# One VectorE transpose of the second input row moved behind the first LayerNorm's statistics, in a two-layer graph kernel on one core

## The chip, the cores and the metric

The kernel runs on one NeuronCore of a Trainium2 chip. A core has five engines that run side by side, each working through its own list of instructions in order: TensorE (matrix products, in the profile PE, its weight loads PEld), VectorE (DVE), ScalarE (ACT), GpSimd (POOL) and SyncE (SP), which here issues the DMA transfers.[...] The metric is the device time of one execution in microseconds (us); all times below are in us unless ns is written.

## What is computed

There are 128 graphs of 128 nodes with 512 features each (`x`), and an adjacency matrix of 128 x 128 for each (`adj`). Two layers follow each other, each with a residual and a LayerNorm without gain:

```python
# layer 0: graph attention, 8 heads of 64 units
feats  = einsum('bnf,hfu->bhnu', X, W)
dense  = leaky_relu(e_self[..., :, None] + e_neigh[..., None, :], 0.2)
att    = softmax(dense + NEG_BIG * (1 - A))
out    = relu(einsum('bhij,bhju->bhiu', att, feats) + b)
x      = layernorm(x + out)
# layer 1: two hypergraph convolutions, Dn H Be H^T (x W^T), with a layer_norm between
h = relu(hypergraph_conv(x, adj, W1, b1))        # 512 -> 1024
h = layer_norm(h, gamma, beta)
y = hypergraph_conv(h, adj, W2, b2)              # 1024 -> 512
x = layernorm(x + (y + x))
```

"The first LayerNorm" below is the one at the end of layer 0.

## The kernel before

The kernel takes two graphs at a time, a pair, so there are 64 pairs (0 to 63); g = 0, 1 is the graph within the pair, called row 0 and row 1 below. The products of the large weight matrices are done in a form with seven half-size products instead of eight (`chain`, line 314; `rows_product`, line 469, whose matmuls stand at L476), and sums of blocks on the other engines.

The order of all instructions is written out by hand. Every step is a small function with a lag and a time; `at` (line 311) and `step` (line 304) collect them. For pair p the step gets the time (p + lag) * 38.6 plus its own, all steps of all pairs are sorted by this number (line 1169), and they are issued in this order. The numbers aren't measured times; they only fix the order on each engine. In the first pairs and the last two, tables (`first`, line 1106, and line 1151) replace some of them. With lags from 0 to 4, a period of the loop works on five pairs at a time: it loads and transposes pair m, makes the features of pair m-1, the attention and first LayerNorm of pair m-2, and so on. A period is named below by the pair whose `propagate` product (pz) begins it.

These are the steps around the change, in the order in which VectorE meets them late in a period:

- `load_blocks` (line 114, L121): SyncE loads the input rows of a pair in 32-row blocks into `xb` (one buffer).
- `x_transpose` (line 370, the instruction is L373): VectorE transposes `xb` into `xT`, one instruction of 128x512 for each row g. GpSimd's `x_sums` (L458, tile xS) and the feature products (pf) read it in the next period.
- `attend` (line 662, L665, tile pav): TensorE's attention products; its weights are eT, which `e_transpose` (L630) makes on VectorE from the loaded blocks eb.
- `attended` (L679, L680): VectorE divides by the softmax sums; `add_bias` (L689): GpSimd adds b0.
- `residual` (L696): VectorE's relu and addition of x; `moments` (L704, L705): statistics and mean and variance, per row.
- `rstds` (L710, L712): VectorE adds epsilon (vea), GpSimd raises to the power -0.5 (rsa), once for both rows.
- `first_shift` and `first_output` (L728, L730, L737): ScalarE applies the LayerNorm.
- `masked` (L579, GpSimd), `leaky` (L595, ScalarE), `largest` (L601, VectorE): the scores of the next pair, behind it.
- `y_sum` (L879 on VectorE, L877 on ScalarE): sums of layer 1's second product, of an earlier pair; one with pyY stands ahead of, one with pyW behind the moved transpose.
- `edges` (L409 to L416) and `r_evict` (L440): VectorE makes hT and the propagation matrix R.
- `propagate` (L760, pz): TensorE multiplies the normalized rows y by R; `z_evict` (L772): ScalarE copies pz to zT, row 0 and then row 1; `z_sums` (L783): GpSimd's four differences zS.
- `hidden` (L795, phX, phY, phW): TensorE's product with W1; its first one reads zT of row 0.
- `h_rstd` (L944 to L947, tile rsh, GpSimd) and `y_scale` (L951, VectorE): the inner layer norm's factor, behind zS on GpSimd.

The steps that the change reorders have these times: `x_transpose` of row 1 has lag 0 and 30.65, from pair 2 on; `residual` of row 1 has lag 2 and 30.7, and `rstds` lag 2 and 30.8. In the same period these belong to pairs m and m-2.

Of the kernel before, what the change touches and what calls it, by code (L numbers as in the profile page):

```python
# [20 lines left out]
def kernel(  # L21
# [289 lines left out]
    def at(lag, time, fn, *args, since=0, until=PAIRS):  # L311
        steps.append((lag, time, fn.__name__, range(since, until), fn, args))
# [63 lines left out]
        )  # L376

    at(0, 26.15, x_transpose, 0, since=2)
    at(0, 30.65, x_transpose, 1, since=2)

    def x_transpose_first(p, s):
        s["px"] = [bank(f"px_{p}_{g}") for g in range(2)]
# [100 lines left out]
    def feature(s, i, to, start):  # L483
# [4 lines left out]
          feature, FW, since=2)  # L488
# [724 lines left out]
```

## Time and profile before

| | |
|---|---|
| median of three runs | 2532.51 (2531.58 to 2532.85) |
| the profiled execution | 2532.93 |
| its span, first to last instruction | 2531.1 |
| granted TensorE clock, mean | 0.998 |
| VectorE, ScalarE, GpSimd busy | 80%, 61%, 71% |
| HBM traffic, mean over the span | 135 GB/s |
| idle of VectorE until xb has landed (L373) | 57.1 in 60 waits |
| idle of GpSimd until vea is there (L712, rsa) | 98.8 in 51 waits |
| idle of ScalarE until the mean is there (L728) | 64.8 in 62 waits |

Idle time of an engine that isn't the bottleneck costs nothing by itself. A period of the loop takes 38.7 from one pz to the next, so 64 pairs with the filling and emptying of the pipeline make up the span. What a change within a period is worth is therefore read from one period's timeline, and multiplied by the number of pairs.

### The profile page before, as it was taken

How to read it: one execution, taken by the hardware profiler on the slowest of the kernel's cores; microseconds unless marked ns; L12 is line 12 of the kernel's file. 1: busy time of each engine (PE TensorE's matmuls, PEld its weight loads, DVE VectorE, ACT ScalarE, POOL GpSimd, SP SyncE). 2: the span in 40 equal slices, each digit the busy share in tenths (PEclk: the TensorE clock that was granted, in tenths of full speed). 3: DMA queues.
4: the chain of work that ended last, by engine and by line, in shares of the span. 5: the costliest groups of instructions: out<-in, count | busy, mean ns of one | idle time of the engine just before them, and what ended most of it. 6: DMA issues, size and time to landing. Idle time of an engine off the chain costs nothing.

```text
span 2531.1 us, 48862 instructions
## 1 busy us (share of the span) xinstructions
PE 2500.8 (99%) x16225; PEld 2253.8 (89%) x16225; DVE 2014.2 (80%) x4580; ACT 1539.8 (61%) x4481; POOL 1794.0 (71%) x2060
## 2 busy tenths in 40 slices
PE   7999999999999999999999999999999999999998
PEld 5898999998999989989989999899899898988997
DVE  7878778778778788787787887887877877778765
ACT  4565665755756656657556566566575565665753
POOL 5767776776677677767776777777677767776774
PEclk9999999999999999999999999999999999999999
DMA  6444445445444444454454544444544444444431
GB/s 186 131 138 137 141 134 147 131 133 142 139 136 140 139 140 140 128 151 130 131 149 130 142 140 139 142 136 128 150 129 135 148 136 137 139 135 142 136 115 51
DMA packets 432747, 345.04 MB, mean 136 GB/s; under 512 B 153176, under 2 KB 382064, under 8 KB 432496
## 3 DMA queue, kind: packets, MB, share of 16 engines
q1 hardware_dynamic: 429024, 337.46, 45.3%
q10 hardware_dynamic: 3472, 4.47, 0.6%
q8 instruction: 129, 2.11, 0.3%
q14 instruction: 122, 1.00, 0.1%
HBM read 239.08 MB, written 102.73 MB: 135 GB/s over the span
## 4 chain that ended last, share of the span: by engine, by line
PE 92%; DVE 2%; DMA 2%; ACT 1%; issue 1%; SPq 1%; POOL 1%; DVEq 0%; POOLq 0%; ACTq 0%
PE phX L795 18%; PE pyX L476 16%; PE phW L795 9%; PE pfX L476 8%; PE pav L665 8%; PE pyW L476 8%; PE phY L795 4%; PE pq L961 4%; PE pz L760 4%; PE pfW L476 4%; PE pyY L476 4%; PE pfY L476 2%; PE pd L432 1%; PE pf L513 1%; DMA xb<-in_x_dram 1%
## 5 line engine op out<-in xcount | busy, mean ns | idle before, releaser
L332 ACT COPY py<-pyX 128x257 f32<-128x257 f32 x189 | 70.6, 374 | 539.4 <-PE pyX L476 523.4
L795 PEld LDWEIGHTS phX<-zS,w_sb 128*128 128x128 f32 x3072 | 363.1, 192 | 32.9 <-issue 31.5
L795 PE MATMUL phX<-zS,w_sb 128*128 128x128 f32 x3072 | 374.3, 275 | 2.3 <-POOL xS L458 1.3
L848 POOL TENSOR_TENSOR sq<-sq 128x512 f32<-128x512 f32 (+2 forms) x384 | 343.4, 894 | 20.3 <-ACT sq L836 0.2
L579 POOL TENSOR_TENSOR nb<-nb,neg 128x512 f32<-128x512 f32 x256 | 318.3, 1276 | 6.9 <-DMA nb<-rd 6.9
L609 ACT ACTIVATE nb<-nb,nm 128x128 f32<-128x128 f32 x1024 | 319.4, 391 | 4.6 <-DVE nm L601 0.4
L595 ACT ACTIVATE nb<-nb,ft 128x128 f32<-128x128 f32 x1020 | 317.3, 389 | 6.8 <-POOL nb L579 6.8
L601 DVE TENSOR_REDUCE nm<-nb 128x4 f32<-128x512 f32 x256 | 174.7, 683 | 174.5 <-ACT nb L595 105.8
L712 POOL TENSOR_TENSOR rso<-veo,mhalf 128x2 f32<-128x2 f32 x63 | 44.1, 700 | 371.2 <-DVE veo L710 371.2
L825 ACT ACTIVATE h<-h,vecs 128x128 f32<-128x128 f32 x768 | 245.0, 392 | 53.6 <-DVE h L810 53.6
L665 PEld LDWEIGHTS pav<-ft,eT 128*128 128x128 f32 x2048 | 243.8, 191 | 17.2 <-issue 12.2
L665 PE MATMUL pav<-ft,eT 128*128 128x65 f32 x2048 | 246.3, 273 | 0.0
L476 PE MATMUL pyX<-w_sb,hS 128*128 128x257 f32 x1008 | 242.5, 382 | 0.0
L476 PE MATMUL pyW<-w_sb,hS 128*128 128x256 f32 x1008 | 238.6, 378 | 1.4 <-DVE y L879 1.4
L476 PE MATMUL pyX<-w_sb,h 128*128 128x257 f32 x1008 | 239.4, 379 | 0.5 <-ACT py L332 0.5
L476 PEld LDWEIGHTS pyW<-w_sb,hS 128*128 128x128 f32 x1008 | 190.6, 189 | 29.1 <-issue 1.8
L689 POOL TENSOR_TENSOR y<-y,b_bc 128x512 f32<-128x512 f32 x128 | 162.6, 1271 | 68.2 <-DVE y L680 68.2
L476 PEld LDWEIGHTS pyX<-w_sb,h 128*128 128x128 f32 x1008 | 186.4, 190 | 25.5 <-ACT py L332 0.9
L476 PEld LDWEIGHTS pyX<-w_sb,hS 128*128 128x128 f32 x1008 | 186.1, 190 | 24.3
L373 DVE STREAM_TRANSPOSE xT<-xb 128x512 f32<-128x512 f32 x124 | 138.0, 1114 | 57.1 <-DMA xb<-in_x_dram 57.1
L951 DVE SCALAR_TENSOR_TENSOR y<-y,rsh,bw_bc 128x512 f32<-128x512 f32 x126 | 148.6, 1218 | 19.0 <-POOL rsh L947 18.5
L630 DVE STREAM_TRANSPOSE eT<-eb 128x512 f32<-128x512 f32 x252 | 162.2, 679 | 0.5 <-DMA eb<-ed 0.4
(174 smaller groups left out, 5726.8 us busy)
## 6 DMA issues: line engine op xcount, KB each, us to landing
nb<-rd SPq DMA_DIRECT2D x127, 512.0 KB
ed<-nb SPq DMA_DIRECT2D x126, 512.0 KB
eb<-ed SPq DMA_DIRECT2D x504, 128.0 KB
x<-in_x_dram SPq DMA_DIRECT2D x64, 512.0 KB
out_dram<-o SPq DMA_DIRECT2D x63, 512.0 KB
xb<-in_x_dram SPq DMA_DIRECT2D x248, 128.0 KB
a<-in_adj_dram SPq DMA_DIRECT2D x64, 128.0 KB
w<-in_adj_dram SPq DMA_DIRECT2D x128, 64.0 KB
```

The source lines that it names most:

```text
L476: nc.tensor.matmul(to[:, :n], lhs[:, k, :], rhs[:, k, :n], start=bool(start) and k == 0, stop=(k == nk - 1), skip_group_check=True,)
L579: nc.gpsimd.tensor_tensor(t, t, neg[:, :, None, :].to_broadcast([P, NB, HH, B]), op=ALU.add)
L595: nc.scalar.activation(t, t, AF.Prelu, bias=s["ft"][:, g, h, 0:1], alpha=SLOPE)
L601: nc.vector.tensor_reduce(s["nm"][:, g, hs], scores(p, s, g, hs).rearrange("p b h j -> p h b j"), AX.XY, ALU.max, negate=True,)
L609: nc.scalar.activation(t, t, AF.Exp, bias=s["nm"][:, g, h:h + 1])
L630: nc.vector.transpose(s["eT"][:, g, hs, :].rearrange("p h (b i) -> p h b i", b=NB), s["eb", g][:, :, hs, :].rearrange("p b h j -> p h b j"),)
L665: nc.tensor.matmul(t[:, h * (U + 1):(h + 1) * (U + 1)], s["eT"][:, g, q * HH + h, :], s["ft"][:, g, q * HH + h, 2:], start=True, stop=True,)
L689: nc.gpsimd.tensor_tensor(s["y"][:, g, :], s["y"][:, g, :], b0_bc, op=ALU.add)
L795: nc.tensor.matmul(to[:, m * N:(m + 1) * N], w[:, k, m * P:(m + 1) * P], rhs[:, k, :], start=bool(start) and m == 0 and k == 0, stop=(k == ...
L825: nc.scalar.activation(dst[:, k, :], src[:, k, :], AF.Relu, bias=b1_sb[:, c:c + 1])
L848: nc.gpsimd.tensor_tensor(t[:, :n, :], t[:, :n, :], t[:, n:2 * n, :], op=ALU.add)
L951: nc.vector.scalar_tensor_tensor(t, t, s["rs", "h"][:, g:g + 1], bw_bc.rearrange("p (j c) -> p j c", j=2), op0=ALU.mult, op1=ALU.add,)
```

## The change

One number: the time of `x_transpose` for row 1 goes from 30.65 to 30.85, which is behind `residual` of row 1 (30.7) and `rstds` (30.8) and ahead of everything that followed them.

```diff
     at(0, 26.15, x_transpose, 0, since=2)
-    at(0, 30.65, x_transpose, 1, since=2)
+    at(0, 30.85, x_transpose, 1, since=2)
```

On VectorE, the four instructions L696, L704, L705 and L710 of pair m-2 now stand ahead of the one L373 of pair m, where they stood behind it. This happens for the transposes of pairs 3 to 63, thus beside the LayerNorms of pairs 1 to 61; pair 2's transpose has its own time in the table `first`, which isn't changed, and pairs 62 and 63 have no transposes beside them. The lists of the other engines stay in the same order.

## The prediction

> **What bounds the kernel now.** I read the page first, then TensorE's list of waits, the timeline of all engines over one ordinary pair (pair 25 of 0 to 63), and last TensorE's timeline at the same two places of other pairs.
>
> ```profile
> PE 2500.8 (99%) x16225; PEld 2253.8 (89%) x16225; DVE 2014.2 (80%) x4580; ACT 1539.8 (61%) x4481; POOL 1794.0 (71%) x2060
> ```
> ```profile
> PE phX L795 <- ACT zT L772: 4.0, 6, 1.6
> ```
>
> TensorE is busy 99% of the span, and the waits put down to it come to some 25 us, nearly all at the two ends of the run. The only one that recurs is the first product of `hidden` (phX) waiting for ScalarE's eviction zT, six times. But a busy matmul record can contain a wait, because its end is modelled, so I go by starts. In this timeline of pair 25 the columns are start, length, engine, line, operation, names, sizes, count and, in brackets, the idle time before with its releaser:
>
> ```profile
> 1018.64 0.42 DVE L879 TENSOR_TENSOR y<-py,pyY 128x257 f32<-128x257 f32 x1
> ...
> 1018.98 1.10 DVE L373 STREAM_TRANSPOSE xT<-xb 128x512 f32<-128x512 f32 x1
> ...
> 1020.01 0.65 DVE L696 SCALAR_TENSOR_TENSOR y<-y,x 128x512 f32<-128x512 f32 x1
> ...
> 1021.64 0.17 DVE L710 TENSOR_SCALAR vea<-mva 128x2 f32<-128x2 f32 x1
> ...
> 1021.89 0.70 POOL L712 TENSOR_TENSOR rsa<-vea,mhalf 128x2 f32<-128x2 f32 x1 [1.92 <-DMA sd<-sr]
> 1022.11 0.42 DVE L879 TENSOR_TENSOR y<-py,pyW 128x256 f32<-128x256 f32 x1 [0.30 <-PE pyW L476]
> ...
> 1025.75 1.95 PE L760 MATMUL pz<-R,y 128*128 128x128 f32 x16
> ...
> 1027.01 1.31 ACT L772 COPY zT<-pz 128x512 f32<-128x512 f32 x2
> ...
> 1027.64 2.05 PE L795 MATMUL phX<-zT,w_sb 128*128 128x128 f32 x16
> ```
>
> The transpose sits ahead of the second residual, and the chain residual, statistics, vea, GpSimd's power, ScalarE's outputs and leaky activations runs without a break into the copy of pz. That copy starts at 1027.01 although the first half of pz (8 of 16 matmuls) is done near 1026.8. So the phX start, 1.89 after pz, is late: first wait, A. A product of this form takes 1.79 from start to start elsewhere in the timeline. The second wait, B, is at the first attention product (pav), which needs VectorE's transposes eT. VectorE, then TensorE:
>
> ```profile
> 1045.61 1.29 DVE L630 STREAM_TRANSPOSE eT<-eb 128x512 f32<-128x512 f32 x2
> ```
> ```profile
> 1046.45 1.97 PE L665 MATMUL pav<-ft,eT 128*128 128x65 f32 x16
> 1048.26 1.11 PE L476 MATMUL pfX<-w_sb,xT 128*128 128x264 f32 x4
> ```
>
> The first of the two eT ends near 1046.3, just before pav starts, and pav takes 1.81 to the next group; the later pav of a pair, whose eT lies ready, takes 1.73 (1013.11 to 1014.84). Now pair 26, then pair 10, where the block load xb landed late:
>
> ```profile
> 1064.47 1.95 PE L760 MATMUL pz<-R,y 128*128 128x128 f32 x16
> 1066.40 0.82 PE L795 MATMUL phX<-zT,w_sb 128*128 128x128 f32 x5
> ...
> 1085.18 1.95 PE L665 MATMUL pav<-ft,eT 128*128 128x65 f32 x16
> 1086.96 1.11 PE L476 MATMUL pfX<-w_sb,xT 128*128 128x264 f32 x4
> ```
> ```profile
> 432.43 1.11 DVE L373 STREAM_TRANSPOSE xT<-xb 128x512 f32<-128x512 f32 x1 [1.64 <-DMA xb<-in_x_dram]
> ...
> 444.20 1.95 PE L760 MATMUL pz<-R,y 128*128 128x128 f32 x16
> 446.64 0.60 PE L795 MATMUL phX<-zT,w_sb 128*128 128x128 f32 x3 [0.49 <-ACT zT L772]
> ...
> 465.42 1.90 PE L665 MATMUL pav<-ft,eT 128*128 128x65 f32 x16
> 467.15 1.11 PE L476 MATMUL pfX<-w_sb,xT 128*128 128x264 f32 x4
> ```
>
> Pair 26: A grows to 1.93, B shrinks to 1.78, and pz to the next pz is 38.70 against 38.72 in pair 25. Pair 10: A is 2.44, B falls to its floor of 1.73, and the period is 39.16 (next pz at 483.36). So what A gains or loses, B gives back until its wait is used up: in ordinary pairs the period is held by B. Its chain is: end of pz, ScalarE's second zT copy (waits for pz, not for statistics), four GpSimd zS differences, the power rsh, VectorE's y_scale at 1032.59, then VectorE almost without a gap to eT.
>
> **What the Trainium skill says.** "Perfetto Trace Analysis", Identifying the Most-Contended Engine: matmul busy share does not tell how close TensorE is to its limit, since its records are pipelined; the 99% above with two hidden waits in it agrees. "SBUF — State Buffer", Who interferes with whom: a VectorE instruction with two SBUF inputs and a GpSimd one that reads SBUF exclude each other, and the first to start holds the port to its end. The trace agrees: the residual of row 0, beside GpSimd's squares, takes 1.34 (at 1014.10), that of row 1 takes 0.65. Pair 62, which has no transposes behind it, has the changed order already, and shows both the price and the effect (GpSimd's m beside the residual, against 0.19 elsewhere; ScalarE's copy):
>
> ```profile
> 2452.47 0.57 POOL L939 TENSOR_TENSOR m<-y 128x1 f32<-128x1 f32 x1 [1.25 <-DVE y L879]
> ```
> ```profile
> 2460.15 0.58 ACT L772 COPY zT<-pz 128x512 f32<-128x512 f32 x1 [0.72 <-PE pz L760]
> ```
>
> There ScalarE waits 0.72 for pz, and phX follows pz by 1.79 (2459.06 to 2460.85): A's floor.
>
> **The change part by part.** No instruction is added or removed; on VectorE one transpose moves behind four instructions (residual, two of statistics, vea) in 61 of 64 pairs, 1 to 61. TensorE, ScalarE, GpSimd and SyncE keep their orders.
>
> 1. *Four instructions earlier.* The residual starts when the transpose did, 1.03 earlier (1020.01 − 1018.98). It needs GpSimd's bias addition, which ends at 1018.81, 0.17 before; so no new wait. GpSimd's two m and the mask (1019.15 to 1019.97) are held by the residual to about 1019.6, end near 1020.5, and are clear of the power, now due near 1020.86. Gain to the power: 1.03; bounds 0.35 (residual doubled to 1.34, as row 0's is) and 1.03.
> 2. *Ordinary pairs, 54.* Everything to the zT copy comes earlier, the copy then waits for pz, A falls from 1.89 to 1.79 as in pair 62, and the phX group behind it, whose first matmul is slow after a wait, from 1.89 (1027.64 to phY at 1029.53) to 1.83 (2460.85 to 2462.68 there): 0.16 to 0.17 in all. B's chain has no link in what moved, so TensorE waits 0.17 longer at pav. Value 0; bounds −9.2 (54 × 0.17, if B gives nothing back) and, upward, the slow rival below.
> 3. *Stretched pairs, five (10, 14, 56, 58, 59).* Periods from pz to pz 39.16, 39.18, 39.16, 39.18, 39.02 against 38.71: 0.45 + 0.47 + 0.45 + 0.47 + 0.31 = 2.15. In each the power is 0.4 to 0.56 later against pz than usual, less than the 1.03 given. Value −2.15; bounds −2.15 and 0 (other late loads could stretch other pairs).
> 4. *Pair 1.* The pipeline is filling: pz at 94.25, phX at 97.82 after 1.62 idle for zT, and pav is at its floor (116.60 to 118.33), so B does not hold it. VectorE idles 1.55 ahead of its h sum there, so what follows can move up. Value −1.03; bounds −1.03 and 0.
> 5. *Pair 61.* VectorE has less to do, pav is at its floor with eT 0.9 early, so A's 0.17 stays gained. Bounds −0.17 and 0.
> 6. *The transpose later.* It now ends near 1021.85 instead of 1020.08. Behind it waits the pyW sum, which TensorE releases at 1022.1 (0.30 idle today): covered, and if that cover were gone R would be late next. Its reader, GpSimd's xS, starts at 1032.53; the next load into xb is issued some 26 us later, so neither SyncE's queue nor any DMA waits for it.
> 7. *GpSimd's masked additions 1.03 earlier.* A small VectorE operation (L415, 0.36 here, 0.17 in pair 1) waits for the running one; the second now ends near 1024.0 instead of the first at 1023.8, so R ends about 0.2 later, near 1024.6. TensorE loads for pz at 1025.53. Free, with 0.9 left.
>
> Sum: 0 − 2.15 − 1.03 − 0.17 = −3.35. From the profiled execution's 2532.93 (span 2531.1 and 1.8 around it) that gives 2529.6. The median of the runs shown is 0.4 below that execution, about one stretched pair fewer; without stretched pairs both come to the same time, so I leave it at 2529.6.
>
> **The rivals.**
> - *Nothing shows* (0.14): late loads stretch as many pairs through other paths and pair 1's gain meets another wait. 2532.5. For it: the xb landing is not touched. Against: the stretched pairs' path leads through the moved instructions.
> - *B does not hold the period* (0.06): A's 0.17 is kept. 2529.6 − 9.2 = 2520.4. For it: A repeats in all pairs. Against: A + B is constant over pairs 25 and 26.
> - *R becomes late* (0.04, slower): the port holds VectorE longer than item 7 says (L415 caught once more, the pyW sum pushed). It costs nothing until 0.9 us is used up; from there each pair pays all of it, since pz is on B's loop. 0.15 over is 61 × 0.15 = 9.2, so 2529.6 + 9.2 = 2538.8.
>
> **How the numbers follow.** The forecast has 0.76, with its own range 2528.3 to 2531.2. A measurement of this kernel can tell about 0.2% (5.1 us) from no change, so 2527.4 to 2537.6 is the same. Faster: 0.06 from the second rival and 0.03 from the forecast's tail. Slower: 0.04. The rest, 0.87, is the same. The range runs from 2526.5 to 2533.0: it takes in "nothing shows" and leaves out the two ends.
>
> **What would show it.** In the changed profile: the power some 1.0 earlier against pz; ScalarE idle ahead of zT; pz to phX near 1.79 in ordinary pairs; the first pav group's wait longer by as much; period still 38.7; no pair near 39.1; pair 1 about 1 us shorter. It is wrong if the period moves by more than 0.03, if pairs are still stretched, or if TensorE waits for R.

## The result, and the profile after

Median 2531.28 (2529.79 to 2531.59, four runs) against 2532.32 (2531.58 to 2532.85, four runs) of the kernel before; the ratio is 0.9995 with a 95% interval of 0.9978 to 1.0012. No difference can be told from these runs. The profiled execution took 2531.51 with a span of 2529.7, against 2532.93 and 2531.1.

First the page of the kernel after (busy time by engine), then two lines of TensorE's waits (engine, line, releaser: microseconds, times, longest):

```profile
PE 2500.1 (99%) x16225; PEld 2251.9 (89%) x16225; DVE 2032.7 (80%) x4580; ACT 1530.5 (60%) x4481; POOL 1818.4 (72%) x2060
```
```profile
PEld pav L665 <- PE pfX L476: 24.1, 57, 0.4
...
PE phX L795 <- ACT zT L772: 0.7, 1, 0.7
```

TensorE's busy time fell by 0.7 only, and phX's waits for zT are gone but for one. The new line is a wait of 0.4 ahead of pav's weight loads, 57 times. It is put down to pfX, which is merely the group that came last; the timeline of pair 25 shows what ended it (the end of VectorE's first eT):

```profile
1018.38 0.69 DVE L696 SCALAR_TENSOR_TENSOR y<-y,x 128x512 f32<-128x512 f32 x1
1018.54 0.57 POOL L939 TENSOR_TENSOR m<-y 128x1 f32<-128x1 f32 x1 [0.34 <-DVE y L879]
...
1020.04 0.17 DVE L710 TENSOR_SCALAR vea<-mva 128x2 f32<-128x2 f32 x1
1020.12 1.09 DVE L373 STREAM_TRANSPOSE xT<-xb 128x512 f32<-128x512 f32 x1
1020.30 0.70 POOL L712 TENSOR_TENSOR rsa<-vea,mhalf 128x2 f32<-128x2 f32 x1 [0.55 <-DVE vea L710]
...
1021.50 0.42 DVE L879 TENSOR_TENSOR y<-py,pyW 128x256 f32<-128x256 f32 x1 [0.29 <-PE pyW L476]
1022.88 0.62 DVE L415 TENSOR_SCALAR deg<-deg 128x2 f32<-128x2 f32 x1
1023.62 0.40 DVE L440 TENSOR_TENSOR R<-pd,dnb 128x256 f32<-128x256 f32 x1
1024.92 1.97 PEld L760 LDWEIGHTS pz<-R,y 128*128 128x128 f32 x16
1025.13 1.95 PE L760 MATMUL pz<-R,y 128*128 128x128 f32 x16
...
1026.22 0.59 ACT L772 COPY zT<-pz 128x512 f32<-128x512 f32 x1 [0.70 <-PE pz L760]
...
1026.92 2.00 PE L795 MATMUL phX<-zT,w_sb 128*128 128x128 f32 x16
1028.75 0.94 PE L795 MATMUL phY<-zT,w_sb 128*128 128x128 f32 x7
...
1044.99 1.29 DVE L630 STREAM_TRANSPOSE eT<-eb 128x512 f32<-128x512 f32 x2
...
1045.83 1.97 PE L665 MATMUL pav<-ft,eT 128*128 128x65 f32 x16
1047.64 1.11 PE L476 MATMUL pfX<-w_sb,xT 128*128 128x264 f32 x4
```

The power now starts 4.83 ahead of pz (1025.13 − 1020.30; before 1025.75 − 1021.89 = 3.86). ScalarE idles 0.70 ahead of the zT copy, and phX follows pz by 1.79. pav still starts when the first of its two eT ends, near 1045.7, and it starts 20.70 after pz, as before (1046.45 − 1025.75 = 20.70).

Mean intervals between starts over the pairs 2 to 60, without the five stretched ones of before, from the two traces:

| from start to start | before (54 pairs) | after (59 pairs) | difference |
|---|---|---|---|
| pz to phX | 1.908 | 1.783 | −0.126 |
| phX to phY | 1.888 | 1.834 | −0.055 |
| last pfX group to pav | 0.898 | 1.090 | +0.192 |
| pav to next pfX | 1.802 | 1.807 | +0.005 |
| the other 22 groups together | 32.211 | 32.211 | 0.000 |
| period | 38.708 | 38.724 | +0.016 |

What wait A gave, B took, and nothing else on TensorE moved. VectorE and GpSimd are busy 18.5 and 24.4 longer than before, with the same instructions: the new neighbours hold each other up (the first m takes 0.58 in the mean instead of 0.20, L415 0.60 instead of 0.39). R, behind L415, still ends 0.9 ahead of its load (1024.02 and 1024.92 above).

No pair of the kernel after is stretched, though its xb was late too, most of all ahead of pairs 55 to 57: in this timeline of pair 57 the first transpose waited 2.11 for the load, the residual behind it and all that follows came 0.67 late, and ScalarE was free for the copy zT just in time.

```profile
2253.01 1.11 DVE L373 STREAM_TRANSPOSE xT<-xb 128x512 f32<-128x512 f32 x1 [2.11 <-DMA xb<-in_x_dram]
...
2260.13 0.70 POOL L712 TENSOR_TENSOR rsa<-vea,mhalf 128x2 f32<-128x2 f32 x1 [0.55 <-DVE vea L710]
...
2264.30 1.95 PE L760 MATMUL pz<-R,y 128*128 128x128 f32 x16
2265.39 0.59 ACT L772 COPY zT<-pz 128x512 f32<-128x512 f32 x1
...
2266.09 2.00 PE L795 MATMUL phX<-zT,w_sb 128*128 128x128 f32 x16
```

The idle time ahead of zT has shrunk from 0.70 to 0.04 (not shown any more by the timeline), the power is 4.17 ahead of pz, and phX is still 1.79 behind pz.

### The profile page after: what moved, and what is told of

The parts are those of the page before. It is cut to its first block, busy times and chain, and to the rows that moved or that the text cites. A ratio compares the mean times of both kernels' runs of the same rounds, so it can differ in the third digit from the quotient of the medians.

```text
span 2529.7 us, 48862 instructions
## 1 busy us (share of the span) xinstructions
PE 2500.1 (99%) x16225; PEld 2251.9 (89%) x16225; DVE 2032.7 (80%) x4580; ACT 1530.5 (60%) x4481; POOL 1818.4 (72%) x2060
## 4 chain that ended last, share of the span: by engine, by line
PE 96%; DMA 2%; POOL 1%; DVE 1%; issue 0%; ACT 0%; SPq 0%; ACTq 0%; POOLq 0%; DVEq 0%
PE phX L795 18%; PE pyX L476 17%; PE pav L665 9%; PE phW L795 9%; PE pfX L476 9%; PE pyW L476 9%; PE pz L760 5%; PE phY L795 4%; PE pfW L476 4%; PE pyY L476 4%; PE pq L961 4%; PE pfY L476 2%; PE pd L432 1%; DMA w<-in_w1t_dram 0%; PE py L1004 0%
## 5 line engine op out<-in xcount | busy, mean ns | idle before, releaser
L848 POOL TENSOR_TENSOR sq<-sq 128x512 f32<-128x512 f32 (+2 forms) x384 | 343.7, 895 | 20.1
L601 DVE TENSOR_REDUCE nm<-nb 128x4 f32<-128x512 f32 x256 | 174.6, 682 | 131.0 <-ACT nb L595 118.8
L373 DVE STREAM_TRANSPOSE xT<-xb 128x512 f32<-128x512 f32 x124 | 137.0, 1106 | 56.8 <-DMA xb<-in_x_dram 56.8
L783 POOL TENSOR_TENSOR zS<-zT 128x256 f32<-128x256 f32 x128 | 93.3, 729 | 112.6 <-ACT zT L772 112.6
```

Of the source, the lines that this page charges most:

```text
L373: nc.vector.transpose(s["xT"][:, g].rearrange("p k (b n) -> p k b n", b=NB), s["xb"][:, g * NB:(g + 1) * NB].rearrange("p b (f k) -> p k b ...
L601: nc.vector.tensor_reduce(s["nm"][:, g, hs], scores(p, s, g, hs).rearrange("p b h j -> p h b j"), AX.XY, ALU.max, negate=True,)
L848: nc.gpsimd.tensor_tensor(t[:, :n, :], t[:, :n, :], t[:, n:2 * n, :], op=ALU.add)
```

## The experiments

The theory is that of the prediction: two hidden waits, A (phX on ScalarE's zT) and B (pav on VectorE's eT), each able to hold the period, so that removing A alone shows only in late pairs and at the ends. Below, A is called at its floor where phX follows pz by 1.78, and B where pav follows the last pfX by 0.89 and takes 1.73, as these groups do when their inputs lie ready. The rivals are that TensorE's own rate holds the period, that A is not a limit in its own right, and that the margin the change gives isn't real. The three groups of runs had medians of 2533.8, 2533.8 and 2533.9 for the kernel before, on which the ratios below stand.

### The change again

> The changed kernel once more. Theory (loop B, from pz over zT row 1, zS, rsh, y_scale to eT, holds the period): period from pz to pz 38.72 to 38.74 again, pz to phX 1.78, no stretched pair, and a time 1.0 to 2.5 us below the kernel before. Rival (the five stretched pairs of the kernel before were chance and the changed kernel's lack of them too): some pairs near 39.1 in this execution, and a time that does not differ from the kernel before.

Measured: 2531.40 (2529.82 to 2531.97, 13 runs) against 2533.83 (25 runs); ratio 0.9991, 0.9982 to 0.9999. The periods are 38.72 to 38.73 again, no pair is stretched, and late loads of pairs 56 and 61 are absorbed. So there is a gain, of some 2.4, a tenth of a per cent: the interval of the ratio just leaves out 1, and the slowest of these 13 runs (2531.97) is faster than the fastest of the 25 (2532.10).

### B removed: the first eT moved ahead of the o normalization

VectorE's first eT is put ahead of the two instructions L715, once in the kernel after and once in the kernel before.

```diff
-        ((0, 0), 31.0, (1, 33.2), (1, 36.1), 4.05, 18.1), ((0, 1), 32.2, (1, 35.0), (1, 36.7), 4.6, 18.15),
+        ((0, 0), 31.0, (1, 33.2), (1, 36.1), 4.05, 16.9), ((0, 1), 32.2, (1, 35.0), (1, 36.7), 4.6, 18.15),
```

> The changed kernel, with the first of the four transposes eT (row 0, first half of the heads) moved ahead of o_norm on VectorE, so that the first pav no longer waits for it. Theory (B holds the period): B's 0.25 us go, ScalarE's 0.70 us ahead of zT shrink to about 0.3 or less since o_norm and with it the xb load come 0.4 later; period about 38.45 to 38.50, time about 2532 - 1.5 - 58 x 0.25 = 2516 us (up to 2522 where A takes part of it back). Rival (TensorE's own rate is the floor, the waits at pav are an artefact of modelled ends): period 38.7, time 2531 us.

> The kernel before, with the same eT moved ahead of o_norm. Theory: B is out of the way, but A has no slack there and its chain (o_norm, output, xb load, transposes, statistics, power, zT) gets 0.4 us longer: period 38.71 - 0.08 + 0.4 = about 39.0, time about 2550 us (2540 to 2560), slower by 0.3 to 1.1%, with pz to phX at 2.2 to 2.4 in every pair. Rival (the transpose's place costs nothing as such): the same gain as in the changed kernel, about 2516 us.

Measured with the change: 2514.99 (2514.18 to 2515.63), ratio 0.9927, 0.9912 to 0.9942. Without it: 2531.8 (2528.99 to 2534.43, 12 runs), ratio 0.9994, 0.9986 to 1.0002. In the kernel after, B's removal is worth 16 us; in the kernel before, nothing that can be told. The weight loads of pav serve as a meter for B (group lines: count, then busy time and mean ns, then idle time before and its releasers). Before, after, and after with the edit:

```profile
L665 PEld LDWEIGHTS pav<-ft,eT 128*128 128x128 f32 x2048 | 243.8, 191 | 17.2 <-issue 12.2 <-DVE eT L642 0.8
```
```profile
L665 PEld LDWEIGHTS pav<-ft,eT 128*128 128x128 f32 x2048 | 243.3, 191 | 29.8 <-PE pfX L476 24.1 <-issue 1.2 <-DVE eT L642 0.8
```
```profile
L665 PEld LDWEIGHTS pav<-ft,eT 128*128 128x128 f32 x2048 | 248.2, 192 | 8.4 <-DVE eT L642 0.8
```

8.4 is the floor (before with the edit, and with the next edit, shows it too). In the kernel after with the edit the timeline still has phX 1.78 behind pz and ScalarE idle ahead of zT:

```profile
1018.39 1.95 PE L760 MATMUL pz<-R,y 128*128 128x128 f32 x16
1019.48 0.59 ACT L772 COPY zT<-pz 128x512 f32<-128x512 f32 x1 [0.57 <-PE pz L760]
...
1020.17 2.00 PE L795 MATMUL phX<-zT,w_sb 128*128 128x128 f32 x16
```

and the median period is 38.447 (mean 38.457; five pairs with late loads have 38.53 to 38.58). In the kernel before with the edit, pav is at its floor in every pair as well, but phX is not, here 1.92 behind pz, with its weight loads waiting:

```profile
1027.76 1.95 PE L760 MATMUL pz<-R,y 128*128 128x128 f32 x16
1029.05 1.28 ACT L772 COPY zT<-pz 128x512 f32<-128x512 f32 x2
1029.68 1.86 PEld L795 LDWEIGHTS phX<-zT,w_sb 128*128 128x128 f32 x16 [0.17 <-ACT zT L772]
1029.68 2.05 PE L795 MATMUL phX<-zT,w_sb 128*128 128x128 f32 x16
```

So A takes over at 38.63, 0.08 below B's 38.71, in 44 of the 59 pairs. The other 15 (2 to 12, 14, 15, 57, 58) are stretched to 39.0 to 39.3 and give the rest back: ahead of twelve of them one of SyncE's four xb issues (L121) lasted 1.4 to 2.1 where 0.45 is the median, and xb landed late.

The expectation for the kernel before was a miss as a whole: A was to be worse by some 0.4 in every pair, since eT now stands ahead of it on VectorE. It came true in those 15 pairs alone, with phX 2.28 to 2.56 behind pz. Most of these late loads go with the edit: in pairs 2 to 8 of the kernel before there is a long issue too (1.2 to 1.4), but it is the fourth of the four, as in all six profiles with loads in time and without the eT edit. In the three with the edit it is the first or second wherever one of these pairs has it. How the edit brings this about stays open. In the other 44 pairs eT cost nothing where it was put. VectorE and GpSimd in the kernel before, then in the one with the edit (o is L715, its squares sq L848):

```profile
1042.34 0.17 DVE L710 TENSOR_SCALAR veo<-mvo 128x2 f32<-128x2 f32 x1
...
1043.26 2.74 POOL L848 TENSOR_TENSOR sq<-sq 128x512 f32<-128x512 f32 x3
1043.33 2.36 DVE L715 TENSOR_SCALAR o<-o,mvo,rso 128x512 f32<-128x512 f32 x2 [0.23 <-POOL rso L712]
1045.61 1.29 DVE L630 STREAM_TRANSPOSE eT<-eb 128x512 f32<-128x512 f32 x2
```
```profile
1044.36 0.17 DVE L710 TENSOR_SCALAR veo<-mvo 128x2 f32<-128x2 f32 x1
...
1045.03 0.71 DVE L630 STREAM_TRANSPOSE eT<-eb 128x512 f32<-128x512 f32 x1
1045.27 2.74 POOL L848 TENSOR_TENSOR sq<-sq 128x512 f32<-128x512 f32 x3
1045.66 2.04 DVE L715 TENSOR_SCALAR o<-o,mvo,rso 128x512 f32<-128x512 f32 x2
```

From the start of veo to the end of the second o it takes 3.35 in the first (1045.69 − 1042.34) and 3.34 in the second, with an eT of 0.71 in between. In the first, VectorE idled 0.23 for rso, and the first o then sat beside GpSimd's first sq, which had started 0.07 ahead of it, for 1.49 in all; in the second, the first o took 1.17. In both it ended 0.28 to 0.29 after that sq. That fits what the Trainium skill says in "SBUF — State Buffer", Who interferes with whom: a tensor_scalar can take the port pair that VectorE shares with GpSimd, and the first to start keeps it. The transpose took 0.71 here, beside the start of sq, and 0.70 elsewhere; it filled the idle time and part of the wait.

### A and B both shortened: the first skip addition ahead of y_scale

`skip` of row 0 (L748, 0.67) stood behind VectorE's y_scale, on the way to eT. At its new place VectorE has idle time (1.26 ahead of its third score maximum L601 in pair 25 of the kernel before).

```diff
-    at(3, 9.3, skip, 0)
+    at(3, 1.05, skip, 0)
```

> The changed kernel, with skip of row 0 (0.9 us of VectorE inside the stretch that A and B share) moved into VectorE's idle time ahead of the third score maximum. Theory: A and B both get 0.9 us, TensorE is left with no recurring wait but A's floor; period 38.45 as in pair 61, time 2531.3 - 58 x 0.27 = about 2515.5 us (2514 to 2520). Rival (TensorE's own rate is the floor already at 38.7): 2531 us.

> The kernel before, with the first of the two skip additions (L748 of row 0) moved from behind VectorE's y_scale to ahead of it, where VectorE waits for GpSimd anyway. Theory: both of the hidden waits lie behind this instruction on VectorE, so taking 0.66 out of that stretch relieves both at once, without the change: pz to phX 1.79, pfX to pav 0.89 and pav 1.73, period 38.45 as in the kernel after with the same edit, 2515 to 2518. Then the change isn't needed for the gain, only something that moves both. Rival: the first wait (A) does not depend on this stretch but on the transpose's place alone; then it stays at 1.89, its group at 1.89, and the period is 38.45 + 0.17 = 38.62, about 2526.

Measured with the change: 2515.95 (2515.31 to 2516.45), ratio 0.9931, 0.9917 to 0.9944, period 38.45. Without it: 2528.74 (2527.96 to 2530.12, 13 runs), ratio 0.998, 0.9972 to 0.9988. The first is as expected. The second went the rival's way: B is at its floor, A stays at 1.92, and the period is 38.65, with two stretched pairs (54 and 58).

The new place has a price. In the second, GpSimd's first zS, which took 0.73, starts in most pairs while the addition runs (VectorE 1027.02 to 1027.70 here) and takes longer:

```profile
1027.16 1.13 POOL L783 TENSOR_TENSOR zS<-zT 128x256 f32<-128x256 f32 x1 [0.82 <-ACT zT L772]
```

So the first eT comes 0.26 earlier against pz in the mean, not 0.67 (20.28 for 20.55), which is still more than the 0.08 by which B's period exceeds A's. Why nothing of it reached A is seen in VectorE's pyY sum, which stands ahead of the transpose and the residual. Its group in the kernel before, and in the one with the edit (idle before it, and its releaser):

```profile
L879 DVE TENSOR_TENSOR y<-py,pyY 128x257 f32<-128x257 f32 x63 | 26.4, 419 | 8.2 <-PE pyY L476 2.2
```
```profile
L879 DVE TENSOR_TENSOR y<-py,pyY 128x257 f32<-128x257 f32 x63 | 26.6, 422 | 19.6 <-PE pyY L476 19.4
```

VectorE, now earlier, waits 0.3 per pair for TensorE's pyY: it is free 7.38 ahead of the next pz instead of 7.16, but the sum starts 7.09 ahead of it instead of 7.06 (means of the ordinary pairs). So A is a loop of its own: TensorE's pyY, the sum, (in the kernel before) the transpose, residual, statistics, vea, power, ScalarE's outputs, zT, phX. Being earlier ahead of pyY doesn't shorten it; taking something out between pyY and phX does. The change takes the transpose out.

With A and B each in place or removed, median times and mean ordinary periods (a period over 38.9 counts as stretched):

| | A in place | A removed by the change |
|---|---|---|
| B in place | 2533.8, 38.708 and 5 stretched pairs | 2531.4, 38.724 |
| B removed by the skip edit | 2528.7, 38.646 and 2 stretched pairs | 2516.0, 38.460 |
| B removed by the eT edit | 2531.8, 38.628 and 15 stretched pairs | 2515.0, 38.457 |

The ordinary period is the longest of three: A's 38.63 to 38.65, B's 38.71 to 38.72, and 38.45, which is what TensorE takes with both waits gone. Whether a further wait hides in the 38.45, none of these runs can tell.

### Both edits with the change

> The kernel after with both edits that made it faster alone: the first eT ahead of the o normalization, and the first skip addition ahead of y_scale. Theory: each edit alone already brought all groups of TensorE to their floors (period 38.446), so there is nothing left for the second: 38.446 to 38.45, 2514.0 to 2516.0. Rival: a further wait is hidden in the floors, and the two gains add: 38.2 to 38.3 and 2500 to 2506.

Measured: 2515.58 (2513.93 to 2516.04), ratio 0.9927, 0.9912 to 0.9941, every period 38.449 to 38.451. The second edit finds nothing left: neither hidden wait holds any more. The three versions, with the change and one or both edits, have ratios of 0.9927 to 0.9931 to the kernel before; the change alone has 0.9991.

### Halfway: the transpose behind the statistics, but ahead of vea

```diff
-    at(0, 30.85, x_transpose, 1, since=2)
+    at(0, 30.75, x_transpose, 1, since=2)
```

> The kernel after, with the row 1 transpose put halfway: behind the second residual and its two statistics, but still ahead of vea, so that the power waits for it as in the kernel before. Theory: what the change gave came from vea's place alone; the power is back at 34.8 to 34.9 behind pz, ScalarE has no idle time ahead of zT, pz to phX is 1.88 to 1.93 and phX to phY 1.89, the first pav group back near 1.78 to 1.81 with pfX to pav at 0.89 to 0.92, period 38.70 to 38.72, stretched pairs above 39.0 are possible again: 2532 to 2534. Rival: the residual's place is what counts (it frees the port for GpSimd's small operations earlier): then pz to phX stays 1.78 and ScalarE idles ahead of zT, 2531.4.

Measured: 2533.32 (2532.22 to 2534.54, 12 runs), ratio 0.9998, 0.9989 to 1.0007. The time is that of the theory, but several of its signs are not: in ordinary pairs pz to phX is 1.78, pfX to pav 1.07 and the period 38.73, about as in the kernel after. Timeline of pair 26 in this kernel:

```profile
1059.44 0.18 DVE L705 BATCH_NORM_AGGREGATE mva<-statsa 128x2 f32<-128x6 f32 x1
1059.54 1.07 DVE L373 STREAM_TRANSPOSE xT<-xb 128x512 f32<-128x512 f32 x1
1060.54 0.13 DVE L710 TENSOR_SCALAR vea<-mva 128x2 f32<-128x2 f32 x1
1060.75 0.70 POOL L712 TENSOR_TENSOR rsa<-vea,mhalf 128x2 f32<-128x2 f32 x1 [1.38 <-DVE vea L710]
...
1064.76 1.95 PE L760 MATMUL pz<-R,y 128*128 128x128 f32 x16
1065.87 0.59 ACT L772 COPY zT<-pz 128x512 f32<-128x512 f32 x1
...
1066.54 2.02 PE L795 MATMUL phX<-zT,w_sb 128*128 128x128 f32 x16
```

The power is 4.01 ahead of pz, 0.15 more than before, which is just more than A's excess of 0.13; ScalarE has no idle time left ahead of zT. So A is at its floor here too, as the rival said, and B gives it back. The margin is missing, though, as the theory said: in pair 56 xb is late, phX starts 2.42 after pz, and the pair is stretched to 39.14, while the kernel after holds against the same lateness (in its pair 56 the power is as late, by 0.67). Pair 1 has no gain either (40.31; 40.29 before and 39.55 after).

So in ordinary pairs the residual's place is enough, and it is worth nothing that can be told. Vea's place adds the rest of the power's lead, 4.83 for 4.01, and what the change gains comes with that lead. It is a margin, not a shorter period. The two times alone don't separate the halfway kernel from the kernel after: their intervals overlap (0.9989 to 1.0007, 0.9982 to 0.9999).

### Late loads in every pair

SyncE issues the xb loads behind the ab loads, in both kernels.

```diff
-            todo.append((16.2 if p == 2 else p * T + 19.0, load_blocks, (p,)))
+            todo.append((16.2 if p == 2 else p * T + 20.6, load_blocks, (p,)))
```

> The kernel before, with SyncE's four xb loads issued behind the four ab loads of the same pair instead of ahead of them; SyncE needs 1.9 us for the ab loads, so xb lands about 2 us later in every pair, more than in the stretched pairs (1.3 to 1.5 late, period plus 0.45). Theory: the lateness goes through the row 1 transpose to the power and zT; all but 0.9 of it is paid: period 39.6 to 39.9, ScalarE never idle ahead of zT, 2585 to 2605 in all. Rival: in steady state the loop shifts and the late load is absorbed: below 2545.

> The kernel after, with the same late loads. Theory: the change gives the power 1.0 us of margin, of which 0.7 is idle time of ScalarE ahead of zT; so 0.7 to 1.0 us less is paid in each of some 60 pairs: period 38.75 to 39.1, 2535 to 2560, thus 40 to 60 below the kernel before with late loads. Rival: the late load is paid through row 0's transpose and the pyY sum, which the change doesn't touch; then both pay the same and the two differ by less than 10.

Measured: before 2600.63 (2597.87 to 2601.32), ratio 1.0262, 1.0245 to 1.0279; after 2549.47 (2548.43 to 2550.17), ratio 1.0061, 1.0046 to 1.0076. They differ by 51.2, or 0.84 for each of 61 pairs. Both times are in the expected ranges, and so are the mean periods (39.85 and 39.03); neither rival came true. Groups of the kernel before with late loads, then of the kernel after with them:

```profile
L373 DVE STREAM_TRANSPOSE xT<-xb 128x512 f32<-128x512 f32 x124 | 137.5, 1110 | 168.5 <-DMA xb<-in_x_dram 168.5
...
L795 PEld LDWEIGHTS phX<-zT,w_sb 128*128 128x128 f32 x1024 | 120.1, 193 | 81.6 <-ACT zT L772 81.6
```
```profile
L373 DVE STREAM_TRANSPOSE xT<-xb 128x512 f32<-128x512 f32 x124 | 136.7, 1103 | 170.8 <-DMA xb<-in_x_dram 170.8
...
L795 PEld LDWEIGHTS phX<-zT,w_sb 128*128 128x128 f32 x1024 | 119.1, 191 | 29.3 <-ACT zT L772 29.3
```

VectorE waits for xb just as long in both (168.5 and 170.8). TensorE's wait for zT is 81.6 in one and 29.3 in the other: 52.3 less, about the difference in time. In the first, pav is at its floor and B gives nothing back; in the second, its meter reads 11.8, near the 8.4 of the floor. This is the change's gain with its cover gone.

The kernel after still pays 18 for the late loads (2549.5 for 2531.4). Row 0's transpose still stands ahead of the pyY sum on VectorE, and that sum starts 1.2 later than usual in both kernels (5.9 ahead of the next pz instead of 7.1), which is more than the margin.

## Why the prediction was right, step by step

The forecast was 2529.6 and no measurable difference; measured were 2531.28 and the same. A difference too small to be told proves little by itself, since the rival "nothing shows" also forecast one; and of the gain of 3.35 that the sum gave, the first comparison showed 1.0 and the repetition 2.4. What speaks for the prediction is that its mechanism held: A falls to its floor, B takes all of it. By its items:

1. *Four instructions earlier* came as worked out: the residual takes 0.69 and isn't doubled, the first m beside it takes 0.57 as in pair 62 of before, and the power gains 0.97 of the 1.03. The halfway kernel splits this: 0.15 comes with the place of the residual and the statistics, the rest with that of vea.
2. *Ordinary pairs*: valued at 0. A gave 0.18 (0.16 to 0.17 forecast), B took 0.197. The 0.016 more per pair is 0.95 over 59 pairs. It was not forecast and repeats in the second profile of the change (38.723); the halfway kernel has 0.022. It lies on B's chain: the first eT ends 20.562 after pz instead of 20.545 in the mean. Of these 0.017, 0.005 are there when y_scale starts (6.848 for 6.843), and the rest gathers in small steps along VectorE's instructions from there to eT. What lengthens them stays open.
3. *Stretched pairs*: −2.15, right: none is left, and late loads that did come were absorbed. There was luck in it too: in pairs 55 to 57 only 0.04 to 0.05 of ScalarE's idle time was left. The runs with late loads show what the change saves on this path, 0.84 per pair.
4. *Pair 1*: mis-sized, −0.74 for −1.03. phX moved from 3.57 to 2.61 behind pz, but B caught there: pfX to pav went from 0.89 to 1.03 and pav from 1.73 to 1.81, together 0.22. That pav was at its floor was taken for a margin; it had 0.74 of it, no more.
5. *Pair 61*: −0.17 forecast, 38.617 to 38.451 measured.
6. *The transpose later*: right; it ends at 1021.21, 3.92 ahead of pz (forecast were 1021.85 and 3.90), and the pyW sum still waits 0.29 for TensorE.
7. *R*: right; L415 takes 0.62, R ends at 1024.02 and is loaded from 1024.92, the 0.9 left that were forecast.

The sum by these is −2.15 + 0.95 − 0.74 − 0.17 = −2.1; the two profiled spans differ by 1.4, because the kernel after reached pz of pair 1 0.71 later (94.96 against 94.25). That stretch scatters by itself: 94.19 in the second profile of the same kernel, and 93.64 to 95.69 over all profiles with loads in time. Of the rivals, "B does not hold" fell with the table of intervals and with the eT edit. "R late" fell with the 0.9. "Nothing shows" is nearest in time, but not in mechanism, since the margin is there and pays 51 us once it is needed.

What the prediction did not see is how near A lay below B: it said that B holds the period, not that removing B alone would be worth so little (38.71 to 38.63), so that the change, worth 2.4 by itself, takes off 13 to 17 once either edit of B is there.

## What to carry to other kernels

A change that removes a real wait can show next to nothing because a second loop, here 0.08 us longer, holds the period: tabulate start-to-start intervals of the bounding engine, and see which interval grew by what another lost. Try the removal of two such waits together before either is dropped as useless, for neither shows its whole worth alone. Where a chain that a late DMA can delay ends at the bounding engine, idle time ahead of its last link is margin: it costs nothing in a quiet run and decides what a late load costs.

## What the hardware showed unexpectedly

- An instruction could be put into another's wait at no cost: eT of 0.71 ahead of o left o's end where it was (3.35 and 3.34 from veo), as the first o took 1.49 beside the squares anyway and 1.17 with eT ahead of it.
- In these traces a VectorE instruction that needs the result of the one before starts about 0.03 after its recorded end (vea, 1020.04, behind the aggregate's 1020.01; the median of the 127 pairs of L705 and vea or veo is 0.035), one that doesn't up to 0.09 ahead of it (the transpose, 1020.12, beside vea's 1020.21; the median of 61 such pairs is 0.092). In the halfway kernel the transpose lies between the aggregate and vea and overlaps both, and the power came 0.15 earlier although the same instructions stand ahead of it as in the kernel before.
- Single xb issues on SyncE last 1.0 to 2.1 instead of 0.45 to 0.48, with loads in time nearly all of them ahead of pairs 2 to 15, and with late loads ahead of pairs 53 to 61; what makes them long stays open. They don't explain all late loads: in the kernel before, pairs 10 and 14 are stretched without a long issue ahead of them, and pairs 2 to 8 have one and aren't stretched.
